# The shift of the second layernorm in layer 2's second step, moved from VectorE to GpSimd

## The chip, the cores and the metric

The kernel runs on one core of a Trainium2 chip. The metric is the device time of one execution in microseconds. Before the change it is 4503.56 us, the median of four runs (4500.06 to 4506.78).

The engines are named as in the profile: PE is TensorE, which multiplies matrices (PEld is its loading of weights), DVE is VectorE, ACT is ScalarE, POOL is GpSimd, and SP is SyncE, which here only starts DMA transfers. Each engine works through its own list of instructions in order; an instruction that waits holds everything behind it on the same engine. ACT and POOL also start DMA transfers, in the same list as their other work.

## The reference

Four graph layers stand one behind another, each followed by a residual sum and a layernorm over the 256 features, on 4096 rows (nodes). The change lies in layer 2, which makes two steps of attention and diffusion and has a layernorm of its own, behind which the common one follows:

```python
for n in range(STEPS):                      # STEPS = 2
    A = _top_p_attention(Xa, W1, W2, W3)
    Xf = R @ Xf
    Xa = A @ Xa
    Z = Z + Xf @ U1[n].T + Xa @ U2[n].T
h = X + Z
...
y = (h - mu) / jnp.sqrt(var + LN_EPS) * ln_g + ln_b      # layer 2's own layernorm
...
x = _layernorm(x + y)                                    # the second layernorm
```

`_top_p_attention` gives the softmax of a bilinear score over all rows, of which each row keeps the largest probabilities up to a sum of 0.9 (the nucleus). `R` is the row-normalized adjacency with the diagonal. `_layernorm(x)` is `(x - m) / sqrt(v + eps)`.

## The kernel before

The 4096 rows are 32 blocks of 128, one row to a partition; blocks are numbered from 0 here. Layer 2 (`layer2`) runs `for step in range(2)`, and in a step over the blocks. For block b, `attention` transposes the masked scores e 128 columns at a time on PE (L1215, four to a copy), ACT copies each four out of PSUM (aT, L1217), and PE multiplies them by X (L1220). `close` adds up the block's terms (L1250 on PE, L1252 on DVE) and, in the second step, makes the two layernorms. `ahead3` computes layer 3's products for the block before (L103, L1284, with part at L121 and L122 and h at L1292). `diffused` (L153, L159) multiplies the next block's rows of the adjacency.

Beside it the scores of the block after next are made (`scores`: L882 on PE, L886 on ACT), ACT evaluates a first guess of the threshold over them (`guessed`; four sweeps ja at L955 over half a row each, and short instructions on 128x1 tiles, fma, which is L894), and DVE refines the threshold for the next block (`nucleus`: two sweeps of L901 over 4096 columns, two of L1033 over 2048 with eight MAX8 each at L1037, then some forty short instructions, and at last the eight L1084 that mask e). A refinement on DVE (L994, L997) needs gw (L986, L988) and sq (L987, L990), which ACT makes beforehand; its first threshold (L1003) needs c, which ACT makes from ja's sums.

The kernel is written in a language whose scheduler fixes the order of instructions on each engine when the program is built, from the order of the source, the dependencies and its own estimate of durations. One edit can so change the order of instructions that it doesn't touch. SP's list holds the loads of the adjacency pieces (L156) and of q (L907) in that stage.

The layernorms use `moments` (L72 to L85): L80 and L81 on DVE give mean and variance, L83 adds eps on POOL, L84 raises to the power -0.5 on POOL. In `close`, with step 1, this stands (L1269 to L1276): moments of h; L1270 and L1271 on DVE apply the first layernorm with its weights and add x; moments again; L1274 makes the shift, -mean times the reciprocal deviation, a 128x1 tile; fma at L1275 (shown as L894, `h<-h,shift,ln_rstd`) makes h times rstd plus shift on ACT; L1276 stores h. So each block has two pairs of L83 and L84 on POOL and one L1274.

Of the kernel before, what the change touches and what calls it, by code (L numbers as in the profile page):

```python
# [17 lines left out]
ALU = mybir.AluOpType  # L18
# [33 lines left out]
class Net:  # L52
# [653 lines left out]
    def layer2(self):  # L706
        nc, tc, NB, D, X, N = self.nc, self.tc, self.NB, self.D, self.X, self.N
        A = 64
        HALF = N // 2
        with ExitStack() as ctx:  # L710
# [82 lines left out]
            def at(b):  # L793
                return bass.ds(b, 1)
# [95 lines left out]
            def small(name, n=1, bufs=2):  # L890
                return work.tile([P, n], F32, name=name, bufs=bufs)

            def fma(out, x, scale, bias, func=AF.Identity):
                nc.scalar.activation(out, x, func, scale=scale, bias=bias)  # L894
                return out
# [191 lines left out]
            def mend(step, e, r):  # L1087


                row = settled()  # L1090
                with tc.If(nc.values_load(row[:, NB:], min_val=0, max_val=1) == 0):
                    with tc.For_i(0, NB - 1, 1) as b:
                        with tc.If(nc.values_load(row[:, at(b)], min_val=0, max_val=1) == 0):
                            e2, Z = exact_scores(b)
                            r2 = exact_nucleus(e2, Z)
                            dif = work.tile([P, 1, D], F32, name="dif")
                            diffuse(dif[:, 0], b)
                            att = work.tile([P, 1, D], F32, name="att", bufs=1)
                            attention(att[:, 0], e2, r2)
                            h = close(step, b, (dif, att))  # L1100
                            if step == 1:
                                ahead3(b, h)
                    with tc.If(nc.values_load(row[:, NB - 1:NB], min_val=0, max_val=1) == 0):
                        e2, Z = exact_scores(NB - 1, e)
                        nc.vector.tensor_copy(r, exact_nucleus(e2, Z))
# [138 lines left out]
            def terms(dst, src, two):  # L1244

                pz = ps1.tile([P, 512], F32, name="ps_r")
                for i in range(2):
                    xT = self.transposed(psum, work, two[i], "xT")
                    for c in range(2):
                        nc.tensor.matmul(pz[:, :D], xT[:, c, :], u[:, i, c, :],  # L1250
                                         start=(i == 0 and c == 0), stop=(i == 1 and c == 1))
                nc.vector.tensor_add(dst, src, pz[:, :D])  # L1252

            def close(step, b, two):

                n = 1 + step
                xb = work.tile([P, 2, D], F32, name="xb", bufs=1)
                nc.scalar.dma_start(xb[:, :n], xd[at(b), :, step:step + n].rearrange("o p s d -> (o p) s d"))
                h = work.tile([P, 1, D], F32, name="h", bufs=2)
                hb = h[:, 0]  # L1260
                if step == 0:
                    nc.scalar.dma_start(xad[at(b)].rearrange("o p d -> (o p) d"), two[1][:, 0])
                    terms(hb, xb[:, 0], two)
                    nc.scalar.dma_start(xd[at(b), :, 1, :].rearrange("o p d -> (o p) d"), hb)
                    nc.vector.tensor_add(xb[:, 1], xb[:, 0], affine)
                    nc.scalar.dma_start(xd[at(b), :, 2, :].rearrange("o p d -> (o p) d"), xb[:, 1])
                else:
                    terms(hb, xb[:, 0], two)
                    mv, rstd = self.moments(work, h)  # L1269
                    nc.vector.scalar_tensor_tensor(hb, hb, mv[:, 0, 0:1], affine, op0=ALU.subtract, op1=ALU.mult)  # L1270
                    nc.vector.scalar_tensor_tensor(hb, hb, rstd, xb[:, 1], op0=ALU.mult, op1=ALU.add)  # L1271
                    mv, rstd = self.moments(work, h)
                    shift = small("shift")
                    nc.vector.scalar_tensor_tensor(shift, mv[:, 0, 0:1], -1.0, rstd, op0=ALU.mult, op1=ALU.mult)  # L1274
                    fma(hb, hb, rstd, shift)  # L1275
                    nc.scalar.dma_start(xo[at(b), :, 0].rearrange("o p d -> (o p) d"), hb)  # L1276
                    return h
# [17 lines left out]
            for step in range(2):  # L1295
# [34 lines left out]
                for b in range(NB):  # L1330
                    if b + 1 < NB:
                        rs[b + 1] = nucleus(*stage[b + 1], evals=1 + step) if b == 0 else None
                    last = b == NB - 1
                    e, r = stage.pop(b)[0], rs.pop(b)
                    if last:
                        if step == 1:
                            ahead3(b - 1, h)
                        mend(step, e, r)

                        n = NB - step  # L1340
                        for k in range(0, n, 4):
                            to = min(k + 4, n)
                            nc.sync.dma_start(XD[:, k:to].bitcast(F32), xfd[k:to].rearrange("b p s d -> p b s d"))
                    att = work.tile([P, 1, D], F32, name="att", bufs=1)
                    attention(att[:, 0], e, r)
                    if step == 1 and 0 < b < NB - 1:
                        ahead3(b - 1, h)
                    h = close(step, b, (difs.pop(b), att))
                    if step == 1 and last:
                        ahead3(b, h, last)  # L1350
                    if 3 <= b + 2 < NB:
                        stage[b + 2] = guessed(scores(b + 2), b + 2, ABOVE[step])
                    if b + 1 < NB:
                        if b:
                            rs[b + 1] = nucleus(*stage[b + 1], evals=1 + step)
                        difs[b + 1] = diffused(b + 1)
# [114 lines left out]
```

## Time and profile before

| What | us |
| --- | --- |
| median of four runs | 4503.56 |
| the profiled execution | 4505.91 |
| its span, first to last instruction | 4504.2 |
| PE busy in the span | 4245.5 |
| DVE busy in the span | 3343.4 |
| ACT busy in the span | 2758.1 |
| POOL busy in the span | 314.5 |
| L1274 on DVE, each of 32 | 0.16 |
| L83 on POOL in this step, each of 64: least, median, most | 0.216, 0.218, 4.478 |
| L84 on POOL in this step, each of 64: least, median, most | 0.555, 0.568, 0.729 |

Times in the traces count from the start of the span. The profile names a group of instructions by line, engine, operation, and output and inputs. Behind an instruction in a timeline stands in brackets how long its engine had been idle before it, and which instruction ended that wait. The 32 closes of layer 2's second step lie between 3033 and 4243 us.

### The profile page before, as it was taken

Reading aid. Unit: us, or ns where it says so; the run is one execution under the profiler, and the core shown is the slowest. Engines: PE = TensorE matmul, PEld = TensorE weight load, DVE = VectorE, ACT = ScalarE, POOL = GpSimd, SP = SyncE. Lnnn points to the kernel's source line nnn. Section 1 sums busy time; section 2 is a strip of 40 time slices with the busy share of each in tenths; the row PEclk is TensorE's granted clock in tenths of the full one; section 3 lists DMA queues with packets and bytes.
Section 4 is the critical chain, followed back from the end, with each engine's and each line's share of the span. In section 5 each row is a group of like instructions: output and inputs, shape, how many; then the busy total and the mean of one; then the engine's idle time right before and its main releaser. Section 6 shows DMA issues by size and latency. Waiting matters only on the chain. (4 is left out here: it accounts for less than half of the span.)

```text
span 4504.2 us, 70573 instructions
## 1 busy us (share of the span) xinstructions
PE 4245.5 (94%) x25625; PEld 3416.7 (76%) x25625; DVE 3343.4 (74%) x7657; ACT 2758.1 (61%) x5501; POOL 314.5 (7%) x538
## 2 busy tenths in 40 slices
PE   8999989999987999999999999887999999999799
PEld 7899989999986876677777777665666666666587
DVE  7632269999994447977777777388989999989354
ACT  5533369998873235866666666257677777676232
POOL 0111100001102100000000000001000000000011
PEclk9999999999998999999999999999999999999899
DMA  4765553332215964022222222530122222222541
GB/s 133 225 196 177 176 201 108 98 136 64 88 36 209 380 236 138 26 79 84 81 80 80 81 79 91 194 116 30 39 79 76 80 79 80 71 68 76 189 142 48
DMA packets 277781, 523.51 MB, mean 116 GB/s; under 512 B 36774, under 2 KB 112294, under 8 KB 273318
## 3 DMA queue, kind: packets, MB, share of 16 engines
q1 hardware_dynamic: 179268, 356.20, 23.9%
q10 hardware_dynamic: 85282, 122.62, 7.9%
q0 software_dynamic: 12864, 39.99, 3.0%
q8 instruction: 207, 3.39, 0.3%
q14 instruction: 160, 1.31, 0.1%
HBM read 363.63 MB, written 155.06 MB: 115 GB/s over the span
## 5 line engine op out<-in xcount | busy, mean ns | idle before, releaser
L1220 PE MATMUL ps_a<-X,aT 128*128 128x256 f32 x4096 | 966.3, 388 | 28.2 <-ACT aT L1217 28.1
L1220 PEld LDWEIGHTS ps_a<-X,aT 128*128 128x128 f32 x4096 | 764.7, 191 | 294.2 <-ACT aT L1217 136.9
L272 PE MATMUL acc<-gm,gt 128*128 128x198 bf16 x8192 | 710.5, 250 | 37.5 <-issue 17.8
L272 PEld LDWEIGHTS <-gt 128*128 128x128 fp8e4 x8192 | 705.4, 98 | 42.6 <-issue 17.9
L264 ACT ACTIVATE sg<-lpb,nlc 128x1024 fp8e4<-128x1024 f32 x640 | 670.5, 1135 | 78.9 <-DVE gt L266 38.9
L479 PE MATMUL pz<-src,ar 128*128 128x264 f32 x4096 | 509.1, 287 | 12.3 <-DVE ar L469 9.9
L159 PE MATMUL ps_r<-XD,adj_piece 128*128 128x512 f32 x2048 | 509.2, 400 | 10.8 <-DMA adj_piece<-adjs 10.3
L479 PEld LDWEIGHTS pz<-src,ar 128*128 128x128 f32 x4096 | 506.1, 189 | 15.2 <-DVE ar L469 12.0
L1217 ACT COPY aT<-ps_tp 128x512 f32<-128x512 f32 x512 | 277.4, 583 | 358.9 <-PE ps_tp L1215 354.6
L955 ACT ACTIVATE ja<-e,nc 128x2048 uint8<-128x2048 f32 x240 | 478.7, 1995 | 0.5 <-issue 0.2
L159 PEld LDWEIGHTS ps_r<-XD,adj_piece 128*128 128x128 f32 x2048 | 382.6, 190 | 110.4 <-DMA adj_piece<-adjs 24.0
L882 PE MATMUL ps_logit<-kT,q 64*128 64x512 f32 x1024 | 462.5, 637 | 4.0 <-ACT e L886 3.9
L901 DVE SCALAR_TENSOR_TENSOR v<-e,c 128x4096 bf16<-128x4096 f32 x100 | 447.2, 4472 | 7.3 <-ACT c L929 6.5
L1037 DVE MAX8 cand<-v 128x8 f32<-128x256 f32 x1024 | 360.7, 412 | 2.2
L1084 DVE SCALAR_TENSOR_TENSOR e<-e,edge 128x512 f32<-128x512 f32 x512 | 347.3, 746 | 1.5
L472 ACT ACTIVATE nb<-a 128x512 uint8<-128x512 f32 x256 | 156.5, 630 | 293.8 <-DMA a<-in_adjt_dram 274.6
L182 ACT ACTIVATE adj_piece<-na 128x1024 fp32r<-128x1024 fp8e4 x128 | 135.2, 1059 | 326.6 <-PE ps_adj L695 135.0
L1215 PE MATMUL ps_tp<-ident,e 128*128 128x128 f32 x2048 | 273.3, 275 | 39.4 <-DVE e L1084 26.1
L1033 DVE SCALAR_TENSOR_TENSOR v<-e,hi 128x2048 f32<-128x2048 f32 x128 | 300.9, 2351 | 1.7
L1215 PEld LDWEIGHTS ps_tp<-ident,e 128*128 128x128 f32 x2048 | 242.1, 142 | 77.8 <-DVE e L1084 29.5
L886 ACT ACTIVATE e<-ps_logit 128x1024 f32<-128x1024 f32 x256 | 261.0, 1020 | 50.0 <-PE ps_logit L882 35.1
L257 DVE TENSOR_SCALAR sg<-lpb,nlc 128x1024 fp8e4<-128x1024 f32 x384 | 273.5, 749 | 1.7
(301 smaller groups left out, 5077.0 us busy)
## 6 DMA issues: line engine op xcount, KB each, us to landing
adj_piece<-adjs SPq DMA_DIRECT2D x512, 256.0 KB
a<-in_adjt_dram SPq DMA_DIRECT2D x256, 256.0 KB
adjs<-adj_piece SPq DMA_DIRECT2D x128, 512.0 KB
na<-nad SPq DMA_DIRECT2D x64, 512.0 KB
na<-nad ACTq DMA_DIRECT2D x32, 1024.0 KB
nad<-nb POOLq DMA_DIRECT2D x128, 128.0 KB, 3.4
lpb<-lpd POOLq DMA_DIRECT2D x32, 512.0 KB, 4.1
xfd<-part ACTq DMA_DIRECT2D x63, 256.0 KB
```

What stands on the lines that cost most here:

```text
L159: nc.tensor.matmul(ps, a[:, k, :], rhs(jc).rearrange("p s d -> p (s d)"), start=(jc == 0 and own is None), stop=(jc == self.NB - 1))
L264: nc.scalar.activation(sg[:, k, :], lpb, AF.Sign, scale=-1.0, bias=nlc[:, jc, h:h + 1], saturate=False)
L272: nc.tensor.matmul(acc[:, q, :6 * C1], gt[:, k, q * P:(q + 1) * P], gm[:, jc, hh, :], start=(jc == 0 and q % 2 == 0), stop=(jc == NB - 1 a ...
L479: nc.tensor.matmul(pz[q][:, t, :W], ar[:, q, k, :], src[:, jc, t, s], start=(jc == 0 and s == 0), stop=(jc == NB - 1 and s == 1))
L882: nc.tensor.matmul(pl[:, s, :], q[s * A:(s + 1) * A, :], kT[s * A:(s + 1) * A, c * 512:(c + 1) * 512], start=True, stop=True)
L901: nc.vector.scalar_tensor_tensor(junk, e, c, e, op0=ALU.is_ge, op1=ALU.mult, accum_out=S)
L955: nc.scalar.activation(ja, e[:, s * HALF:(s + 1) * HALF], f, bias=nc1, accum_out=fs[:, i + s:i + s + 1])
L1033: nc.vector.scalar_tensor_tensor(v, ec, hi, ec, op0=ALU.is_lt, op1=ALU.mult, accum_out=sb[:, s:s + 1])
L1037: nc.vector.max(cand[:, 8 * j:8 * j + 8], v[:, k * 256:(k + 1) * 256])
L1084: nc.vector.scalar_tensor_tensor(ec, ec, edge[:, j:j + 1], ec, op0=ALU.is_ge, op1=ALU.mult)
L1215: nc.tensor.transpose(pt[:, k * P:(k + 1) * P], e[:, jc * P:(jc + 1) * P], self.ident)
L1220: nc.tensor.matmul(pa[:, :D], aT[:, k * P:(k + 1) * P], X[:, jc, :], start=(jc == 0), stop=(jc == NB - 1))
```

## The change

One instruction is issued to another engine. The shift is computed by POOL, with a scalar from the tile rstd and the constant -1, instead of by DVE:

```diff
                     mv, rstd = self.moments(work, h)
                     shift = small("shift")
-                    nc.vector.scalar_tensor_tensor(shift, mv[:, 0, 0:1], -1.0, rstd, op0=ALU.mult, op1=ALU.mult)
+                    nc.gpsimd.tensor_scalar(shift, mv[:, 0, 0:1], rstd, -1.0, op0=ALU.mult, op1=ALU.mult)
                     fma(hb, hb, rstd, shift)
                     nc.scalar.dma_start(xo[at(b), :, 0].rearrange("o p d -> (o p) d"), hb)
                     return h
```

It stands in `close` and is executed once for each of the 32 blocks in the second step (a further copy stands in `mend`, whose blocks are only run when a check of the thresholds asks for it). The built program's order of instructions on DVE, ACT, PE, POOL and SP differs from the one before in layer 2's second step.

## The prediction

> **What bounds the kernel now.** I read the page first, then the stretches of layer 2's second step, then the tile that changes, then the timeline around it.
>
> ```profile
> span 4504.2 us, 70573 instructions
> PE 4245.5 (94%) x25625; PEld 3416.7 (76%) x25625; DVE 3343.4 (74%) x7657; ACT 2758.1 (61%) x5501; POOL 314.5 (7%) x538
> ```
>
> The profiled execution lasted 4505.91 us, 1.7 of it outside the span, and 2.35 above the median of the four timed runs (4503.56). TensorE is the busiest engine, but the edit lies in one stage of some 1200 us, so that stage has to be read alone. Columns: stretch, its length, then busy time (and count) of PE, PEld, DVE, ACT, POOL, the granted clock, and DMA:
>
> ```profile
> 2990.00:3107.00 117.00, 103.51 (x445) 73.47 (x446) 110.74 (x300) 80.00 (x212) 6.77 (x10) 0.94 0.13 42
> 3107.00:3185.00 78.00, 51.42 (x218) 35.46 (x216) 64.52 (x181) 48.35 (x129) 6.76 (x6) 0.82 0.06 19
> 3185.00:3458.00 273.00, 264.02 (x1125) 184.29 (x1124) 251.32 (x664) 193.82 (x505) 21.30 (x28) 0.99 0.21 69
> 3458.00:4121.00 663.00, 639.93 (x2755) 449.46 (x2754) 615.11 (x1608) 475.66 (x1231) 29.35 (x68) 1.00 0.24 76
> ```
>
> From 3185 on, PE is busy 97% (639.93 of 663): a block of 128 rows takes 39.0 us there and PE sets it. Before that, in blocks 0 to 3, VectorE (110.74 of 117) sets the pace, and PE stands still for 25.8 us. The tile of the edit, in the view of one tile (min/median/max ns; then waits in us, times):
>
> ```profile
> L1274 DVE SCALAR_TENSOR_TENSOR shift<-ln_mv,ln_rstd x32: 158/160/161, 3043.6 to 4242.0; 128x1 f32<-128x1 f32 x32
>   DVE shift L1274: 47.5, 25
>   POOL ln_rstd L84: 22.2, 32
> ```
>
> DVE loses 22.2 us waiting for the deviation; ACT waits 47.5 us for the shift. The timeline in block 2 shows the rest (start, duration, [idle before]):
>
> ```profile
> 3107.13 0.17 DVE L81 BATCH_NORM_AGGREGATE ln_mv<-ln_stats 128x2 f32<-128x6 f32 x1
> 3107.33 4.47 DVE L901 SCALAR_TENSOR_TENSOR v<-e,c 128x4096 bf16<-128x4096 f32 x1
> 3107.39 1.05 ACT L1217 COPY aT<-ps_tp 128x512 f32<-128x512 f32 x2
> 3107.39 4.48 POOL L83 TENSOR_SCALAR ln_var<-ln_mv 128x1 f32<-128x1 f32 x1 [1.34 <-DVE ln_mv L81]
> 3111.95 0.57 POOL L84 TENSOR_TENSOR ln_rstd<-ln_var,power 128x1 f32<-128x1 f32 x1
> 3112.55 0.16 DVE L1274 SCALAR_TENSOR_TENSOR shift<-ln_mv,ln_rstd 128x1 f32<-128x1 f32 x1 [0.75 <-POOL ln_rstd L84]
> 3112.75 0.60 ACT L894 ACTIVATE h<-h,shift,ln_rstd 128x256 f32<-128x256 f32 x1 [1.48 <-DVE shift L1274]
> 3122.27 0.22 DVE L994 SCALAR_TENSOR_TENSOR d<-S,S,gw 128x1 f32<-128x1 f32 x1 [9.56 <-ACT gw L988]
> 3158.09 1.97 PE L1215 MATMUL ps_tp<-ident,e 128*128 128x128 f32 x8 [25.81 <-DVE e L1084]
> ```
>
> Two things are seen. L83, elsewhere 0.22 us, lasted 4.48 because it began 0.06 us after L901 and ended when that did. And the order of ACT decides when gw (L988) comes; DVE waits 9.56 us for it, and PE waits for DVE's e.
>
> **The change part by part.**
> *Removed from DVE:* 32 x 0.16 = 5.1 us of work and the 22.2 us wait: 27.3 us, 0.85 a block. From block 4 on it lies beside PE, which is 97% busy; without that cover it would be a gain of 28 x 0.85 = 24 us.
> *Added to POOL:* 32 TENSOR_SCALARs of 128x1. With a scalar from a tile the form is not in the trace. L83, the same operation with a constant, takes 0.22; L84 beside it 0.57; held, L83 takes 4.48. I take 0.25 plus 0.06 for the start, and the bounds 0.22 and 4.48 where DVE's next long instruction decides. DVE no longer stops there, so that now has to be asked. In the changed program's order the second L81 is followed at once by L901 in block 3, and within 0.6 us by L1033 in blocks 7 to 10; shift can start only 1.03 us after L81 (0.09 + 0.22 + 0.08 + 0.57 + start), so it is held about 4 us in block 3 and 2 us in those four. In blocks 1, 2 and 5 L83 is held as before; in the others MAX8s follow, under which L83 lasted its 0.22.
> The row against a rule: at 4010.75 L1033 began 0.23 us after L84 and lasted 2.35 as everywhere, so POOL does not slow DVE, and this costs 0. The Trainium skill (SBUF — State Buffer, Who interferes with whom) says that whichever of the two starts first keeps the shared port for its whole instruction. By it a shift in front of an L1033 could hold DVE too, an estimate of 32 x 0.25 = 8 us; half of the rule, POOL waiting for DVE, is what L83's 4.48 shows.
> *Moved on ACT:* the program is ordered anew, and h (L894), which now waits for POOL, stands earlier: in block 0 ahead of an aT copy, in block 1 ahead of an aT and a ja, in block 2 ahead of an aT pair and a ja, in block 5 ahead of a ja. Behind h on ACT then stand the aT that feeds PE's next matmuls, and the ja and gw that feed DVE. Walked with the rows' durations:
> Block 0: aT goes from 3042.48 to 3044.45, so the matmuls of 3043.09 start at 3045.1 (+2.0); the next group waited 2.01 anyway, which leaves +0.8, and L122 on DVE (3064.44), which waits for ACT behind PE, keeps it: the 0.85 is lost again.
> Block 1: L83 is held 2.29 by L1033, h starts at 3079.85, ACT idles 3.2, and aT, the z's and a ja (4 us) now stand behind it. part (L121, 3094.70) comes at +4.4. DVE reached L122 2.9 us after part was there, so +4.4 becomes +1.45.
> Block 2: h at 3112.75 + 1.45 + 0.15 = 3114.35, aT at 3114.85 instead of 3107.39. Behind it: three aT pairs (3.1), DMA issues (0.7), w to few (0.9), three ja (6.3), small ones (1.9), an e (1.0): gw at 3128.5, and L994 at +6.3.
> Block 3: -0.85 for the shift; h, held by L901, 4.0 later, makes gw late again for the next L994, by 1.6. L1084's e ends at +6.9, and PE restarts at 3165.0 instead of 3158.09: **+6.9**.
> Blocks 5 and 7 to 10: h sits under the 8 us of L159's 32 matmuls, which need nothing of ACT. In block 12 of before, aT waited only 0.18 us for PE, so of 2 us some 1 reaches PE: block 5 moves a ja (2.1), and 7 to 10 lose 2 us against blocks that were not held, of which 7, 8 and 9 were held before too. I take 2 + 2 = **+4**, bounds 0 and 5 x 2 = 10.
> Later blocks: shift ready about 0.15 us later, under L159: 0. DVE's lead takes off some of PE's waits for L1252 (2.1 us of 3200 to 4160, 7.5 on the weight queue): **-1**, bounds 0 and -9.6.
> *Last block:* one chain: shift takes 0.25 + 0.06 on POOL instead of 0.19: +0.1. SP: two loads of q change place with pieces of adj; both land long before use: 0.
> **Sum:** 6.9 + 4 - 1 + 0.1 = +10. On the profiled 4505.91 that is 4515.9; on the median, 4513.6.
>
> **The rivals.**
> *A, DVE is what paces PE, and its 27 us show (not slower).* For it: DVE is 93% busy in the steady stretch. Against it: DVE waited 19.1 us for ACT's c between 3200 and 4160, so it runs ahead. PE's waits there on ACT and DVE sum to 25.0 us (12.9 aT, 6.4 and 0.4 xT, 2.9 and 2.1 h, 0.3 e); half of them and 4 x 0.85 from blocks 0 to 3 give -16: 4488. It decides once DVE's freed time brings gw and e forward by more than h holds ACT, that is if L994's wait stays under 9.56.
> *B, nothing shows.* ACT is busy 72% in the steady stretch, so its idle time takes up the holds, and in block 2 PE's waiting for e (25.8) swallows the late aT. Against it: gw, not aT, is what DVE waits for. 4503.6, give or take 4.
> *C, the new order starves PE once more.* One gap like that of 3132 to 3158, in blocks 7 to 9, where DVE already waited 7.46 for c: 25.8, and 2.2 more for slow matmuls after it (1.97 and 5.04 instead of 1.04 and 3.72): 4531.6. Against it: from block 13 the new order repeats the old one of three blocks later.
> That the change does nothing can't be: the program has no L1274 on DVE and all on POOL.
>
> **How the numbers follow.** A measurement here tells about 0.2%, 9 us, from nothing. The forecast 4513.5 gets 0.57; its own range is 4505 to 4524 (the bounds of the +4 and the -1, and 3 for the walk), of which two thirds, 0.38, lie above 4512.6 and 0.19 within. A 0.17, B 0.12, C 0.14. Faster 0.17, same 0.31, slower 0.52. The range leaves out the far half of A and part of C: 4492 to 4530.
>
> **What would show it.** Right: h's wait on ACT, now for POOL, is over 5 us in block 2, L994's wait in that block is some 13 to 16 us, PE's restart after its 25-us gap comes 5 to 9 us later, and L1274 on POOL lasts over 4 us in block 3. DVE's 22.2 us are gone, and PE's busy share from 3458 on is the same within 1%. Wrong: a restart at 3158 or earlier, a steady block under 38.7 us, or another gap of PE over 10 us.

## The result and the profile after

The changed kernel takes 4515.75 us, the median of 35 runs (4506.34 to 4523.94), against 4505.66 us for 56 runs of the kernel before on the same chips: a ratio of 1.0023, 95% interval 1.0018 to 1.0028, or 10.1 us more. The profiled execution of the changed kernel took 4511.42 us, only 5.5 more than the profiled one before; that difference is taken up below.

The page of the changed kernel, its span and busy times:

```profile
span 4509.7 us, 70556 instructions
PE 4254.2 (94%) x25625; PEld 3423.2 (76%) x25625; DVE 3344.1 (74%) x7625; ACT 2760.6 (61%) x5501; POOL 330.3 (7%) x570
```

POOL has 32 instructions more and VectorE 32 fewer. VectorE's busy time did not fall by 32 x 0.16: in the step its instructions do add up to 3.8 us less, but they overlap each other less. The same stretches as before (stretch, length, then busy time and count of PE, PEld, DVE, ACT and POOL, granted clock, DMA):

```profile
2990.00:3107.00 117.00, 102.50 (x427) 72.12 (x428) 107.37 (x289) 76.31 (x205) 8.13 (x10) 0.91 0.13 42
3107.00:3185.00 78.00, 49.19 (x206) 35.18 (x204) 58.51 (x158) 46.71 (x117) 12.35 (x10) 0.80 0.06 18
3185.00:3458.00 273.00, 260.49 (x1113) 183.11 (x1111) 255.99 (x676) 194.61 (x504) 22.50 (x35) 0.99 0.21 69
3458.00:4121.00 663.00, 650.49 (x2781) 455.03 (x2780) 611.77 (x1587) 475.69 (x1228) 34.34 (x85) 1.00 0.23 76
```

From 3107 to 3185 every engine but POOL did less than before (VectorE 58.51 instead of 64.52), and in the stretch ahead of it too (107.37 instead of 110.74): time is lost there. From 3458 on PE is busy 650.49 instead of 639.93 of 663: time is won there. So the change costs in the first blocks and pays part of it back later. In the view of one tile, the shift and who waits for it:

```profile
L1274 POOL TENSOR_SCALAR shift<-ln_mv,ln_rstd x32: 264/265/2424, 3042.0 to 4246.6; 128x1 f32<-128x1 f32 x32
  POOL shift L1274: 63.6, 23
```

ACT's wait for it has grown from 47.5 to 63.6 us. The timeline shows what that does in block 2 (start and duration stand ahead of each instruction):

```profile
3109.69 4.47 DVE L901 SCALAR_TENSOR_TENSOR v<-e,c 128x4096 bf16<-128x4096 f32 x1
3109.75 4.48 POOL L83 TENSOR_SCALAR ln_var<-ln_mv 128x1 f32<-128x1 f32 x1 [1.34 <-DVE ln_mv L81]
3114.98 0.27 POOL L1274 TENSOR_SCALAR shift<-ln_mv,ln_rstd 128x1 f32<-128x1 f32 x1
3115.28 0.60 ACT L894 ACTIVATE h<-h,shift,ln_rstd 128x256 f32<-128x256 f32 x1 [5.16 <-POOL shift L1274]
3115.79 0.56 ACT L1217 COPY aT<-ps_tp 128x512 f32<-128x512 f32 x1
3117.63 1.99 ACT L955 ACTIVATE ja<-e,nc 128x2048 uint8<-128x2048 f32 x1
3129.22 0.22 DVE L994 SCALAR_TENSOR_TENSOR d<-S,S,gw 128x1 f32<-128x1 f32 x1 [15.05 <-ACT gw L988]
3166.42 0.90 PE L1215 MATMUL ps_tp<-ident,e 128*128 128x128 f32 x3 [24.72 <-DVE e L1084]
```

L83 was held 4.48 us by L901 before too. New is that ACT stands still for 5.16 us ahead of h with the aT copies and the ja still to do; then gw is late, VectorE waits 15.05 us at L994 where it waited 9.56, and PE restarts at 3166.42 instead of 3158.09. Two more places, block 0 and block 3:

```profile
3041.97 2.35 DVE L1033 SCALAR_TENSOR_TENSOR v<-e,hi 128x2048 f32<-128x2048 f32 x1
3042.03 2.42 POOL L1274 TENSOR_SCALAR shift<-ln_mv,ln_rstd 128x1 f32<-128x1 f32 x1
3044.49 0.60 ACT L894 ACTIVATE h<-h,shift,ln_rstd 128x256 f32<-128x256 f32 x1 [3.60 <-POOL shift L1274]
...
3145.46 4.47 DVE L901 SCALAR_TENSOR_TENSOR v<-e,c 128x4096 bf16<-128x4096 f32 x1
3145.54 4.82 POOL L84 TENSOR_TENSOR ln_rstd<-ln_var,power 128x1 f32<-128x1 f32 x1
3150.46 0.27 POOL L1274 TENSOR_SCALAR shift<-ln_mv,ln_rstd 128x1 f32<-128x1 f32 x1
3150.76 0.60 ACT L894 ACTIVATE h<-h,shift,ln_rstd 128x256 f32<-128x256 f32 x1 [5.21 <-POOL shift L1274]
```

In block 0 the shift itself is held, by an L1033 that started 0.06 us earlier; in block 3 it is L84. Before, VectorE stood waiting for the deviation at these points, and so could not start the long instruction that now holds POOL.

**A ruler for the stages.** Executions begin layer 2's second step at times up to 8 us apart (2982.8 to 2991.2 in the 14 profiles of this study), so each profile is measured from its own marks: S, where PE's weight loads (PEld) stop for 9 to 10 us ahead of the step's first L153; R, the first matmul after PE's gap of some 25 us; E, where the weight loads stop for some 11 us ahead of layer 3's products. R-S so covers blocks 0 to 3, E-R the rest of the step. In us against the kernel before (whose R-S is 170.5, E-R 1087.8, E-S 1258.3):

| kernel | R-S | E-R | E-S | time: ratio to before, 95% interval |
| --- | --- | --- | --- | --- |
| before, a second profile (e12) | 0.0 | +0.2 | +0.3 | |
| changed | +10.3 | -3.6 | +6.7 | 1.0023 [1.0018, 1.0028] |
| POOL from block 4 (e1) | +0.7 | -4.6 | -3.9 | 1.0003 [0.9994, 1.0012] |
| POOL in blocks 0 to 3 (e2) | +10.8 | -0.8 | +9.9 | 1.0030 [1.0018, 1.0042] |
| POOL, and a copy on VectorE (e3) | +1.7 | +0.9 | +2.6 | 1.0009 [1.0000, 1.0018] |
| two shifts (e4) | +13.5 | +11.7 | +25.2 | 1.0057 [1.0044, 1.0071] |
| ACT's old order, blocks 0 to 2 (e5) | +5.0 | -3.8 | +1.2 | 1.0006 [0.9997, 1.0015] |
| the same, blocks 1 and 2 (e6) | +4.0 | -2.5 | +1.5 | 1.0011 [1.0002, 1.0020] |
| no shift (e7) | +9.0 | -8.3 | +0.8 | 1.0003 [0.9994, 1.0013] |
| block 0 on VectorE (e9) | +8.4 | -3.8 | +4.6 | 1.0012 [1.0003, 1.0021] |
| the same, and old order (e10) | +0.5 | -2.9 | -2.4 | 0.9990 [0.9981, 0.9999] |
| POOL from block 11 (e11) | 0.0 | +27.3 | +27.3 | 1.0063 [1.0049, 1.0077] |

For the changed kernel this accounts for 6.7 us of the 10.1 (interval 8.1 to 12.6), and for 0.8 more in layer 3 (from E to the span's end 259.1 us instead of 258.3). Some 2.6 us between profile and medians are not attributed; the profiled execution of the changed kernel lay 4.3 us under its median.

The column E-R bears less than one pair of profiles suggests: the changed kernel, e1, e5, e6, e9 and e10 have the same order on ACT from R on and the same shifts on POOL, and yet lie between -2.5 and -4.6.

### The profile page after: what moved, and what is told of

Same layout as the page of the kernel before. It is cut to its first block, busy times and chain, and to the rows that moved or that the text cites. A ratio compares the mean times of both kernels' runs of the same rounds, so it can differ in the third digit from the quotient of the medians.

```text
span 4509.7 us, 70556 instructions
## 1 busy us (share of the span) xinstructions
PE 4254.2 (94%) x25625; PEld 3423.2 (76%) x25625; DVE 3344.1 (74%) x7625; ACT 2760.6 (61%) x5501; POOL 330.3 (7%) x570
## 5 line engine op out<-in xcount | busy, mean ns | idle before, releaser
L1220 PE MATMUL ps_a<-X,aT 128*128 128x256 f32 x4096 | 969.1, 389 | 33.1 <-ACT aT L1217 33.1
L1220 PEld LDWEIGHTS ps_a<-X,aT 128*128 128x128 f32 x4096 | 767.7, 192 | 296.7 <-ACT aT L1217 132.6
L901 DVE SCALAR_TENSOR_TENSOR v<-e,c 128x4096 bf16<-128x4096 f32 x100 | 447.2, 4472 | 7.3 <-ACT c L929 6.5
L1084 DVE SCALAR_TENSOR_TENSOR e<-e,edge 128x512 f32<-128x512 f32 x512 | 347.0, 745 | 1.5 <-DVE d L996 0.2
L1033 DVE SCALAR_TENSOR_TENSOR v<-e,hi 128x2048 f32<-128x2048 f32 x128 | 301.0, 2352 | 1.9
L1215 PEld LDWEIGHTS ps_tp<-ident,e 128*128 128x128 f32 x2048 | 242.9, 143 | 77.1 <-DVE e L1084 28.1
```

The source lines that it names most:

```text
L901: nc.vector.scalar_tensor_tensor(junk, e, c, e, op0=ALU.is_ge, op1=ALU.mult, accum_out=S)
L1033: nc.vector.scalar_tensor_tensor(v, ec, hi, ec, op0=ALU.is_lt, op1=ALU.mult, accum_out=sb[:, s:s + 1])
L1084: nc.vector.scalar_tensor_tensor(ec, ec, edge[:, j:j + 1], ec, op0=ALU.is_ge, op1=ALU.mult)
L1215: nc.tensor.transpose(pt[:, k * P:(k + 1) * P], e[:, jc * P:(jc + 1) * P], self.ident)
L1220: nc.tensor.matmul(pa[:, :D], aT[:, k * P:(k + 1) * P], X[:, jc, :], start=(jc == 0), stop=(jc == NB - 1))
```

## The experiments

All diffs are against the changed kernel. An edge of order, as used below, only says that one instruction of an engine's list stands behind another.

### Which blocks: e1, e2

```diff
-                    nc.gpsimd.tensor_scalar(shift, mv[:, 0, 0:1], rstd, -1.0, op0=ALU.mult, op1=ALU.mult)
+                    if not isinstance(b, int) or b >= 4:
+                        nc.gpsimd.tensor_scalar(shift, mv[:, 0, 0:1], rstd, -1.0, op0=ALU.mult, op1=ALU.mult)
+                    else:
+                        nc.vector.scalar_tensor_tensor(shift, mv[:, 0, 0:1], -1.0, rstd, op0=ALU.mult, op1=ALU.mult)
```

> Shift on POOL in blocks 4 to 31 only, on VectorE in blocks 0 to 3; in the program's order ACT's work around h in blocks 0 to 4 is that of before, from block 5 on that of the changed kernel. Theory (the loss is made in blocks 0 to 3, by h standing earlier on ACT and waiting for POOL's shift there; from block 4 on PE paces and some 3 us are won back): PE restarts after its 25-us gap as in before, DVE's wait at L994 is about 9.6 us, and the time is 4500 to 4505 us, that is 1 to 5 us under before. Rival 1 (each shift on POOL costs the same, 10.1/32 = 0.32 us): 28 x 0.32 = +8.8, 4514.5. Rival 2 (the loss is made by the new order in blocks 5 to 13): +10, 4515.7.

For e2 the condition is `isinstance(b, int) and b < 4`.

> Shift on POOL in blocks 0 to 3 only, on VectorE in blocks 4 to 31; ACT's order is that of the changed kernel in blocks 0 to 4 and that of before from block 5 on. Theory: PE restarts 7 to 10 us later than in before against the step's start, DVE's wait at L994 is 14 to 16 us, nothing is won back later because VectorE stops for the deviation again, and the time is 4512 to 4517 us. Rival 1 (0.32 us for each shift on POOL): 4 x 0.32 = +1.3, 4507. Rival 2 (order of blocks 5 to 13): no change, 4505 to 4507.

e1: 4505.44 us against 4504.93 for the kernel before, measured beside it, ratio 1.0003; restart +0.7, VectorE's wait at L994 10.63 us. The loss is gone with POOL's shift in 28 blocks, which ends the rival of a fixed price for each. The forecast gain of 1 to 5 us shows in the profile (E-S -3.9) and not in the medians, so the expected time is missed, by 0.4 us. e2: 4517.05 us, restart +10.8, L994 waits 14.90 us, and nothing is won back (E-R -0.8): four shifts make all of the loss ahead of the restart, as the theory had it.

### Order or instruction: e3, e4

```diff
+                    sp = small("sp")
-                    nc.gpsimd.tensor_scalar(shift, mv[:, 0, 0:1], rstd, -1.0, op0=ALU.mult, op1=ALU.mult)
+                    nc.gpsimd.tensor_scalar(sp, mv[:, 0, 0:1], rstd, -1.0, op0=ALU.mult, op1=ALU.mult)
+                    nc.vector.tensor_copy(shift, sp)
```

> POOL makes the shift in all 32 blocks, and VectorE copies it for h (L894); the program's order on ACT around h in blocks 0 to 9 is then that of before but for two small exchanges (block 0: one aT behind h as before, block 3: dxb ahead of h), and VectorE stops for the shift as it did for the deviation. Theory (order, not POOL's instruction, costs the time in blocks 0 to 3): the shift comes some 0.35 us later in each block than in before, PE restarts 0 to 3 us later, and the time is 4505 to 4510 us. Rival 1 (POOL's instruction is what costs): at least as slow as the changed kernel, 4516 to 4526.

e3: 4509.25 us against 4504.93, ratio 1.0009; restart +1.7, L994 waits 9.56 us. VectorE stops for the copy, so its long instructions never run under POOL's shift (none of the 32 lasted over 0.3 us), and ACT's order up to block 9 is the old one but for one place in block 3: with POOL making every shift the large loss does not come.

e4 makes the shift twice, the second into the tile that h uses:

```diff
+                    sp = small("sp")
+                    nc.gpsimd.tensor_scalar(sp, mv[:, 0, 0:1], rstd, -1.0, op0=ALU.mult, op1=ALU.mult)
                     nc.gpsimd.tensor_scalar(shift, mv[:, 0, 0:1], rstd, -1.0, op0=ALU.mult, op1=ALU.mult)
```

> The changed kernel with the shift made twice by POOL in all 32 blocks (the second is the one h uses); ACT's and VectorE's order is that of the changed kernel. Theory: 0.3 us more ahead of h in each of blocks 0 to 3, hidden from block 4 on, so 0 to 3 us above the changed kernel: 4515 to 4519 us. Rival 1 (the POOL instruction itself costs 0.32 us a block, or holds VectorE's port): twice the loss, 4524 to 4528.

4528.71 us, 13 above the changed kernel: the theory's 0 to 3 is a miss, and the rival's 4524 to 4528 is nearly hit. The profile shows no fixed price, though. The restart is 3.2 later than in the changed kernel, as expected; 9.5 us come in blocks 4 to 10. Block 4's timeline:

```profile
3206.58 0.28 POOL L1275 TENSOR_SCALAR sp<-ln_mv,ln_rstd 128x1 f32<-128x1 f32 x1
3206.84 2.35 DVE L1033 SCALAR_TENSOR_TENSOR v<-e,hi 128x2048 f32<-128x2048 f32 x1
3206.84 2.39 POOL L1276 TENSOR_SCALAR shift<-ln_mv,ln_rstd 128x1 f32<-128x1 f32 x1
3209.27 0.60 ACT L894 ACTIVATE h<-h,shift,ln_rstd 128x256 f32<-128x256 f32 x1 [2.93 <-POOL shift L1276]
```

Here the second shift falls under L1033, and h starts 3.76 us after L81's end, 1.36 in the changed kernel. In blocks 7 to 10 it is 3.76 instead of 2.89, because L84 is held there (2.72 us): it starts some 0.05 us after L1033, and 0.04 us in the changed kernel, where it takes its 0.57. Measured from S, L1252 (which ends each block's sum) is 3.7 us behind the changed kernel in block 4, 13.2 in block 11 and 18.2 in block 31. "Hidden from block 4 on" was wrong: from block 4 to block 10 h's come 6.4 us later in all, and L1252 falls back by 9.5. Of the 5 us after block 11 the cause is not known; between blocks 12 and 28 the granted clock was 0.99 instead of 1.00 and PE waited 2.4 us longer for pieces of the adjacency.

### ACT's order put back: e5, e6

The programs' lists for ACT around h of block 2 (few and far, w: short instructions; store: L1276; dxb: the load of xb):

```
before    ja  dxb  aT aT  w few w far few  ja  [h]  far  store  aT aT  ja
changed   ja  [h]  aT  store  aT  dxb  w few w far few  ja  far  ja  aT aT
```

In e5 and e6 h keeps waiting for POOL's shift in all 32 blocks, but stands in blocks 0 to 2 (e6: 1 and 2) where it stood in the kernel before. The core of the edit (the numbers are the sweep of `guessed(b + 3)`, and in e5 for block 0 the third aT of the next attention, behind which h is put):

```diff
+                            turn += 1
+                            if b - 3 in hold and turn == {1: 1, 2: 2}.get(b - 3):
+                                tc.add_manual_dep(hold.pop(b - 3), ins.name, mybir.DependencyInfo(mybir.DependencyClass.NoSync, mybir.DependencyReason.DATA))
...
-                    fma(hb, hb, rstd, shift)
+                    ins = nc.scalar.activation(hb, hb, AF.Identity, scale=rstd, bias=shift).ins
+                    if isinstance(b, int) and b in (0, 1, 2,):
+                        hold[b] = ins
```

> The changed kernel (shift on POOL in all 32 blocks), with h (L894) of blocks 0, 1 and 2 tied by an edge of order alone behind an aT copy, a first ja and a second ja, so that ACT's order in blocks 0 to 2 is that of before and in all later ones that of the changed kernel. Theory (h ahead of aT and ja on ACT in blocks 0 to 2 is what costs): PE restarts 0 to 2 us later than in before against the step's start, and the time is 4500 to 4507 us, like the kernel with POOL from block 4 on. Rival 1 (the shift on POOL, held by VectorE's two-input instructions, costs wherever ACT's h stands): 4511 to 4516.

> As the run with ACT's old order in blocks 0 to 2, but block 0 keeps the changed kernel's order (h ahead of an aT), where the shift was held 2.42 us by L1033. Theory: block 0 alone makes the restart 2.5 to 4 us later (the changed kernel lost 3.4 us between block 0's and block 1's L1252), and the time is 3 us above that run, 4504 to 4510. Rival (block 2 alone makes the loss, as the prediction had it nearly): the time of that run within 1 us.

e5: 4508.07 us against 4504.76 (1.0006); restart +5.0. e6: 4508.43 (1.0011); restart +4.0, L994 waits 10.66 us. So the order is worth some 6 us of the 10.3, but the restart expected of e5 (0 to 2) and its time (4500 to 4507) are misses: something else is left. And block 0's order is worth nothing that shows: e6 has the new one there and is no later than e5. So the rival of e6 has the number right (that of e5 within 1 us), but not its reason, block 2 alone: what is left comes by block 1. Measured from S, its L1252 is 3.3 (e5) and 4.0 us (e6) late, and in both h of block 0 starts 3.52 us after L81 as in the changed kernel, behind the held shift. The order is not the old one everywhere: in both kernels a ja stands ahead of an aT pair behind h of block 2, where the kernel before has the pair first.

### Without the shift: e7

```diff
-                    shift = small("shift")
-                    nc.gpsimd.tensor_scalar(shift, mv[:, 0, 0:1], rstd, -1.0, op0=ALU.mult, op1=ALU.mult)
-                    fma(hb, hb, rstd, shift)
+                    fma(hb, hb, rstd, cs[:, 0:1])
```

> The shift is left out: h (L894) takes a ready constant as its bias, so the mean is not subtracted in the last layernorm; ACT's order stays that of the changed kernel (but in block 1 h stands one aT earlier). Theory: block 0's hold (2.4 us) and those of blocks 7 to 10 (1.8 us each) go, h still waits in blocks 1 to 3 for a deviation that L83 or L84 makes while VectorE holds it, so PE restarts 5 to 8 us later than in before, and the time is 4505 to 4512 us. Rival 1 (it is the shift's instruction on POOL that costs, not ACT's order): the restart is that of before within 1 us, and the time 4498 to 4504.

e7 leaves the mean in its result and serves for the time alone: 4504.98 us against 4504.76. Block 1's L1252 is +0.4 late instead of +3.7, so block 0's loss was the held shift. The restart is still +9.0, with no shift in the program at all: h waits for the deviation that L83 makes late under L901, and stands ahead of ja and aT. L994 and the restart:

```profile
3125.54 0.22 DVE L994 SCALAR_TENSOR_TENSOR d<-S,S,gw 128x1 f32<-128x1 f32 x1 [15.98 <-ACT gw L988]
3162.38 1.97 PE L1215 MATMUL ps_tp<-ident,e 128*128 128x128 f32 x8 [24.36 <-DVE e L1084]
```

After the restart it wins 8.3 us where the changed kernel wins 3.6. ACT's order is the same there up to block 13, and but for one or two places in five later blocks, so the 4.7 between them is, within the 2 us that E-R bears, the price of POOL's shift behind R; the L1252s show it in blocks 5 to 11 (6.6 us by block 11).

### The two causes apart: e9, e10

e9 is the changed kernel with block 0's shift on VectorE (condition `not isinstance(b, int) or b >= 1`), e10 adds e6's edges for blocks 1 and 2.

> The changed kernel, with block 0's shift on VectorE as before; ACT's order in block 0 is then that of before, in blocks 1 and 2 and later that of the changed kernel. Theory after eight runs (two separate causes in blocks 0 to 3: the shift of block 0 held 2.4 us by L1033, which is +3.7 by block 1, and h ahead of ja and aT on ACT in blocks 1 and 2, which alone makes the restart 9 us later, as without a shift): L1252 of block 1 within 1 us of before, PE's restart still 8 to 10 us later, time 4511 to 4516. Rival (the causes add up: 10.3 - 3.7): restart 6 to 7 us later, time 4508 to 4511.

> Block 0's shift on VectorE, POOL's from block 1 on, and h of blocks 1 and 2 tied by an edge of order behind a first and a second ja, so that ACT's order in blocks 0 to 2 is that of before. Theory: what was left in the two runs with old order (+4.0 and +5.0 at the restart) was block 0's held shift; now the restart is 0 to 2 us later than in before, and the time 4501 to 4506. Rival (POOL's shift in blocks 1 to 3 costs of itself): restart 3 to 5 us later, 4506 to 4509.

e9: 4511.44 us against 4506.13 (1.0012), restart +8.4. e10: 4503.90 (0.9990), restart +0.5. Both theories held. L994 (L1000 in e10) and the restart of e9:

```profile
3130.95 0.22 DVE L994 SCALAR_TENSOR_TENSOR d<-S,S,gw 128x1 f32<-128x1 f32 x1 [16.84 <-ACT gw L988]
3167.37 1.97 PE L1215 MATMUL ps_tp<-ident,e 128*128 128x128 f32 x8 [26.40 <-DVE e L1084]
```

and of e10:

```profile
3120.46 0.22 DVE L1000 SCALAR_TENSOR_TENSOR d<-S,S,gw 128x1 f32<-128x1 f32 x1 [10.64 <-ACT gw L994]
3156.89 1.97 PE L1221 MATMUL ps_tp<-ident,e 128*128 128x128 f32 x8 [26.41 <-DVE e L1090]
```

These two programs run the same instructions on the same engines, and in this step the lists of PE, VectorE, POOL and SP are the same; in ACT's, two h with their stores (and one load of xb) stand elsewhere. The waits differ by 6.2 us, the restarts by 7.9, the medians by 7.5. In block 2 h starts 5.62 us after L81 in both: the shift is as late in the one as in the other, and only what stands behind h on ACT tells whether that costs anything. That is the cause of the larger part, shown. The causes don't add up: the held shift of block 0 is worth 3.5 us at the restart with the old order (e6 against e10), 1.9 with the new (changed kernel against e9). These two pairs are less clean: without the held shift the scheduler also puts block 2's aT pair ahead of the ja again. At block 1's L1252, ahead of that, the held shift costs 3.2 and 3.1 us; that the wait at L994 takes some of it in with the new order is likely, and not shown.

e10 is the fastest kernel of the study, 2.2 us ahead of the one before; its interval, 0.9981 to 0.9999, only just leaves out no change.

### Two attempts at more: e8, e11

e8 gives POOL the whole last normalisation:

```diff
-                    shift = small("shift")
-                    nc.gpsimd.tensor_scalar(shift, mv[:, 0, 0:1], rstd, -1.0, op0=ALU.mult, op1=ALU.mult)
-                    fma(hb, hb, rstd, shift)
+                    nc.gpsimd.tensor_scalar(hb, hb, mv[:, 0, 0:1], rstd, op0=ALU.subtract, op1=ALU.mult)
```

> POOL makes the whole normalisation of h (subtract the mean, multiply by the deviation, 128x256) in one instruction; there is no shift, and ACT has no h (L894). An estimate from L700 (0.76 us for 128x256 on POOL): 0.8 us, up to 5 where VectorE holds it. Theory: nothing on ACT or VectorE waits for POOL's second deviation any more, h is needed only a block later, so ACT's idle time ahead of h (before: 0.8, 0, 1.5 us in blocks 0 to 2) and its 0.6 us go: restart 1 to 5 us earlier than in before, time 4494 to 4503 us. Rival 3 (a longer POOL instruction gets in VectorE's way, or comes late for the next block's transposes of h): not under 4505.

4583.08 us, 1.0168 [1.0154, 1.0182]: 78 us slower, as the rival had it (not under 4505), and "nothing on ACT or VectorE waits for POOL's second deviation any more" was wrong. ACT's list still holds the store of h:

```profile
3564.76 4.47 DVE L901 SCALAR_TENSOR_TENSOR v<-e,c 128x4096 bf16<-128x4096 f32 x1
3565.41 4.92 POOL L1273 TENSOR_SCALAR h<-h,ln_mv,ln_rstd 128x256 f32<-128x256 f32 x1
3570.36 0.34 ACTq L1274 DMA_DIRECT2D xo<-h  x1
3570.75 0.20 ACT L1005 ACTIVATE low<-c 128x1 f32<-128x1 f32 x1 [11.38 <-POOL h L1273]
```

L1005 needs nothing of POOL; the DMA issue ahead of it in the list does, and ACT stood for 11.38 us. In nine places that is 101.4 us. (L1273 takes 1.24 us where nothing holds it; the estimate from L700 was 0.8.)

e11 takes the condition `b >= 11` of e1's edit, to keep the old program where POOL's shift cost and win what the later blocks won.

> Shift on POOL in blocks 11 to 31 only, on VectorE in blocks 0 to 10, where ACT's order is that of before. Theory (POOL's shift costs in blocks 5 to 10, where VectorE's L1033 holds it 1.8 us, and VectorE's freed time gains 6 to 7 us after block 11): against the step's start block 11 as in before within 1.5 us, the step's end 5 to 7 us earlier, time 4497 to 4503. Rival (the later blocks' gain is only the spread of single executions): 4503 to 4507.

4536.68 us, 31 more than before: a miss on both sides. Up to block 12 it is the kernel before within 1 us; from block 17 to 31 it loses some 2 us a block. The scheduler has gone over to another repeating order there, in which, from block 20 to 28, every second block's shift falls under L901 (3.94 to 4.07 us). One of them:

```profile
4068.59 4.46 DVE L901 SCALAR_TENSOR_TENSOR v<-e,c 128x4096 bf16<-128x4096 f32 x1
4069.24 3.94 POOL L1275 TENSOR_SCALAR shift<-ln_mv,ln_rstd 128x1 f32<-128x1 f32 x1
4073.22 0.60 ACT L894 ACTIVATE h<-h,shift,ln_rstd 128x256 f32<-128x256 f32 x1 [8.37 <-POOL shift L1275]
```

ACT waits 77.1 us for 17 of the 21 shifts. The expectation rested on its order up to block 12. How much is the hold and how much the rest of the new order was not separated.

### The ruler: e12

> The kernel before once more, unchanged, for a second profile of it: how far two executions of one program differ in the times from the step's start to PE's restart and from there to the step's end. If these stay within 1 us, the stage differences of 3 us and more between the kernels are theirs; if they differ by 3 or more, the stage readings of single profiles bear no more than that. Time 4499 to 4511.

The kernel before again, 4504.8 us in one run: R-S and E-S are those of the first profile within 0.3 us. Inside the steady part single blocks are up to 2.3 us apart, so by this pair the table's columns carry differences of 1 us (E-R some 2, as said there), and one block's place about 3.

## Why the prediction was right in its sum, and where its steps were not

**The bound and the place.** Right. The loss lies in blocks 0 to 3 of the second step, and the larger part of it comes by the chain that was named: L83 under L901, h late on ACT, gw late, L994, L1084, PE's restart (e2, e9 against e10).

**Nothing to be had from VectorE's 27.3 us beside PE.** Not settled: the later blocks did win time, and whether VectorE's made it stays open (below). Rival A is out: L994's wait went to 15.05 instead of staying under 9.56.

**+6.9 in blocks 0 to 3** measured +10.3. The step that failed is block 0: "the 0.85 is lost again" took the shift there to be free, and L1033 holds it 2.42 us. The list of held shifts was read off the order of the program ("block 3", "blocks 7 to 10"), with 1.03 us from L81 to the shift's start; in block 0 the shift started 1.06 us after L81, 0.06 behind L1033, too near for a walk by hand. The list also lacked block 29, where L1033 holds the shift 2.10 us without a loss that shows. By L1252, counted from S, the loss grew to +3.7 after block 0 (forecast 0), +4.6 after block 1 (+1.45), +9.8 after block 2 (+6.3 at L994), +10.3 at the restart (+6.9). The steps after block 0 were of the right size: 6.6 where 6.9 was said. In block 3 "h, held by L901, 4.0 later" came true by L84 (4.82 us, h's wait 5.21), not by L1274; in e9 and e10 it is the shift there, 4.57 and 4.58 us. Two small slips of the working: what is listed behind block 2's aT brings gw to 3128.75, not 3128.5, and 6.3 - 0.85 + 1.6 is 7.05, not 6.9.

**+4 for blocks 5 and 7 to 10.** The size is right: 4.7 between changed kernel and e7, and in the changed kernel itself the loss grew by 3.1 us from R to block 11's L1252 (5.3 against e12). The shift was held 1.79 us in each of blocks 7 to 10, as said. That block 5's ja, moved behind h, makes half of it was not tested: e7 has it in the same place.

**-1 for the later blocks** is the term that was mis-sized most: from block 11 to E the changed kernel won 6.7 us (9.4 against e12), and e7, without the price of the shift, won 8.3 from R on, near the far bound of -9.6. PE's waits for aT at L1220 between blocks 12 and 28 fell from 7.1 to 0.8 us. Whether VectorE's freed time or ACT's new order from block 5 on did it stays open: e1 and e9 have both and win 4.6 and 3.8, e2 (old order, VectorE stops) 0.8, e3 (the old order up to block 9, then one of its own; VectorE stops) nothing, and e11, which was to separate them, changed its order again.

**The sum.** The forecast 4513.5 lies 2.3 us under the median, and 2.1 of these are the kernel before, 4505.66 over 56 runs instead of 4503.56 over four: as a change, +10 was forecast and 10.1 measured. By stages it was 6.9 + 4 - 1 against 10.3 + 4.7 - 8.3 = 6.7, with the rest outside the step or not attributed: two terms were off by 3.4 and 7.3 us in opposite senses. That agreement is luck in good part. The low end of the forecast's own range doesn't follow from its bounds either: 6.9 + 0 - 9.6 + 0.1 - 3 = -5.6 gives 4498, not 4505.

**Rivals.** B asked that ACT's slack take up the holds: from block 11 on the changed kernel indeed lost nothing, before it did. C's new gap of PE over 10 us didn't come; the largest new one is 4.84 us, at block 0's L1220. An order that costs far more than the forecast is possible all the same: e8 and e11 lose 78 and 31 us, though by many waits and not by one gap.

**The signs.** Right: h's wait in block 2 (5.16), L994's (15.05), the restart 8.3 us later on the clock, VectorE's 22.2 gone. Wrong: L1274 over 4 us in block 3 (0.27; it was L84), and PE's share from 3458 on, which rose from 96.5 to 98.1%, more than the 1% allowed.

## What to carry to other kernels

An instruction that is moved to an idle engine is only as early as that engine's other waits let it be; what counts is which in-order list the consumer stands in, and what stands behind it there. Taking a short wait out of a busy engine also lets its next long instruction start earlier, and that may be just what holds the helper engine. And when a scheduler orders the program, compare its lists before and after for the whole loop, not the first third: the same instructions in another order were worth 7.5 us here, and an edit that kept the change out of blocks 0 to 10 cost 31.

## What the runs showed of the hardware

**POOL waited for VectorE's long two-input instructions; where POOL was first, VectorE hardly waited.** L901 and L1033 read e twice (as both tensor inputs). An instruction of POOL that starts 0.06 to 0.72 us after one of them does not end before it, whichever it is: L83 4.48, L84 4.82 (elsewhere 0.57), L1274 2.42 and 1.79, and in e8 the 128x256 L1273 4.92. At 0.01 to 0.05 us it went either way: the shift 4.57 in block 3 of e9 and 2.39 in block 4 of e4, and L84 2.72 in blocks 7 to 10 of e4, but L84 0.57 in blocks 7 to 10 of the changed kernel. Under MAX8s L1273 kept its 1.24.

The other way round, in e8 an L1033 began 0.40 us into a 1.24-us L1273 and lasted 2.35 as everywhere; another, begun 0.26 us into one, 2.44:

```profile
3114.94 1.24 POOL L1273 TENSOR_SCALAR h<-h,ln_mv,ln_rstd 128x256 f32<-128x256 f32 x1
3115.34 2.35 DVE L1033 SCALAR_TENSOR_TENSOR v<-e,hi 128x2048 f32<-128x2048 f32 x1
...
3242.40 1.24 POOL L1273 TENSOR_SCALAR h<-h,ln_mv,ln_rstd 128x256 f32<-128x256 f32 x1
3242.66 2.44 DVE L1033 SCALAR_TENSOR_TENSOR v<-e,hi 128x2048 f32<-128x2048 f32 x1
```

In e8 and e11 sixteen L901 began up to 0.14 us into an L84, lasted 4.46 to 4.48, and left L84 its 0.57.

The Trainium skill (SBUF — State Buffer, Who interferes with whom) says that a VectorE instruction with two inputs in SBUF contends with a POOL instruction that reads SBUF, and that the first to issue keeps the shared pair for its whole instruction while the other blocks. The first half is what the holds show. The second half, with POOL first, these runs don't bear out: of the 0.84 and 0.98 us that L1273 still had to run, VectorE lost 0 and 0.08 (L1033's median is 2.352, the later of the two took 2.435).

**Two executions of one program agree within 0.3 us over a step of 1258 us** (the kernel before and e12), while its start moved by 1.3 us between them and by up to 8 us among the kernels.
